# A transformer block on one core: the order of sums at a unit's end, the place of the first weight loads of an item, and the shape of the last part

## The chip, the cores and the metric

The kernel runs on one core of one Trainium2 chip. Its time is the device time of one execution in microseconds (us). The core has five engines that work side by side, each through its own instructions in order: TensorE (PE in the profile; its weight loads are PEld), VectorE (DVE), ScalarE (ACT), GpSimd (POOL) and SyncE (SP). POOL, SP and ACT also issue DMA transfers, each on its own queue. Engines wait for each other by semaphores; an instruction that waits holds up all that stand behind it on its engine.

## The reference

One transformer block with conditioning, for 2 batch items of 2048 tokens with C = 576 channels, 16 heads of 36 channels, all in float32:

```python
ada = silu(c) @ W_ada + b_ada
shift_msa, scale_msa, gate_msa, shift_mlp, scale_mlp, gate_mlp = split(ada, 6)
h = layernorm(x) * (1 + scale_msa) + shift_msa
q, k, v = split(h @ W_qkv + b_qkv, 3)               # 16 heads of 36
x = x + gate_msa * (softmax(q @ k.T / 6) @ v @ W_proj + b_proj)
h = layernorm(x) * (1 + scale_mlp) + shift_mlp
x = x + gate_mlp * (gelu(h @ W_fc1 + b_fc1) @ W_fc2 + b_fc2)   # 2304 hidden columns
```

## The kernel before

**Front.** The modulation, and the queries, keys and values of batch item 0, are computed first and stored to scratch tensors in device memory (`qk_d`, `v_d`). Gates are multiplied into W_proj and W_fc2, which also go to scratch. This takes some 330 us and the change doesn't touch it.

**Attention units.** The main part is a loop over 128 units: 8 blocks of 512 query tokens (4 for each batch item) times 16 heads. A unit has four groups g = 0 to 3 of 512 keys. One step G of the loop does, for groups of different units that overlap: `scores` (16 matmul instructions into two PSUM tiles `s`, L496) and their copy into `e` by ScalarE (`keep`, L509); `exps` (L555, ScalarE); the subtraction of the row maximum `m` (`less`, L551, VectorE); the running maxima `acc` (L514, VectorE); and `weigh`, the values (L567), which sums into the one PSUM tile `av`. Scores are eight groups ahead of values. At g = 0 TensorE turns the finished maxima of a later unit (`turn`, `mt`, L532), VectorE reduces them (`mx`, L542), and SP stores and loads them as `m`. At g = 3 `take` moves `av` out of PSUM: ScalarE copies one half into `up` (L579) and VectorE adds the other (L580). Only then can the next unit's first `weigh` write `av`. A step later `store` writes `up` to `o_d`, half by SP and half as an accumulating DMA by POOL (L588, L589), which waits for SP's to land.

**Other work.** Between scores and values a step may take one piece of other work from a list (`fill`), written as generators. A counter of matmul time (`credit`) decides whether a step takes one: at even g always, at odd g when the credit is over 2.55. The list holds first the projections of batch item 1 (`projections`, four items, `pq` L770 and `pv` L732), then for each of the 8 blocks, once its 16 heads are done, `block(k)`: the output projection into `po` (`begin(k)`, L887) with the residual sum into `x_b` (L899) and layer norm statistics (L102, L103), the first MLP matmuls `pf` (`up_to`, L970 and L956), gelu in three parts (`gT` L981, then L990 and L992, then the later half L998 and L1000, deferred by a list `later` that `flush` works off), and the second MLP matmuls in three parts `down(0)` to `down(2)` of four row tiles each (`py`, L1020), summed into `x_b` (L1032) and at the end stored (L1035). `begin(k + 1)` runs inside `block(k)`, between the last `pf` and `down(2)`, if its heads are done. A piece's PSUM result is moved out by a closure that `fill` returns in `dones`. At the end of a step the order is: `take` if g = 3, then `flush`, then `dones`.

**PSUM and buffers.** While attention runs, other work uses two PSUM banks (`ps_f`); a po, py or pv row tile takes both, one for each half of its 576 columns, and the next such tile waits until the sums have freed them. After attention, `room` gives the two tiles of the scores out as well. `up` and `av` have one buffer each. The weights of `pq` and of `pf` share two buffers (tag `w1`); one set of 256 columns is three DMAs on POOL's queue (`load_cols` with L613, L614, L616; `load_w1` with L867 and twice L870). `x_b` tiles are loaded by POOL (`load_x`, L636), four DMAs for a block.

**The lines around the change.** `projections` loads its first two weight sets when its item begins; `block` loads its first two when the block begins, behind `begin`. The last unit ends near 3592 us; what follows is other work alone, the remainder of block 6 and block 7.

Of the kernel before, what the change touches and what calls it, by code (L numbers as in the profile page):

```python
# [22 lines left out]
def dit_block_kernel(  # L23
# [408 lines left out]
    with ExitStack() as main_part:  # L432
# [175 lines left out]
        def load_cols(key, w, bias, lo, n):  # L608

            t = mp.tile([P, KC, 2 * P], F32, tag="w1", name=f"w1_{key}_{lo}")  # L610
            main, last = pieces(w)
            cols = ds(lo, n)
            seq(nc.gpsimd.dma_start(out=t[:, 0 : KC - 1, :n], in_=main[:, :, cols]))  # L613
            seq(nc.gpsimd.dma_start(out=t[0:KL, KC - 1, :n], in_=last[:, cols]))  # L614
            seq(
                nc.gpsimd.dma_start(out=t[KL : KL + 1, KC - 1, :n], in_=bias[cols].unsqueeze(0))  # L616
            )
            return t
# [71 lines left out]
                yield cost if lights else 1.0, take  # L690

        made = {}

        def tokens(b, tb):

# [14 lines left out]
        def projections(b, tb):  # L710

            key = f"q{b}_{tb}"
            wv = load_square("v", (w_qkv[:, 2 * C :], b_qkv[2 * C :].unsqueeze(0)))
            pairs = [(m, min(2, 2 * C // P - m)) for m in range(0, 2 * C // P, 2)]
            ws = {m: load_cols(key, w_qkv, b_qkv, m * P, n * P) for m, n in pairs[:2]}
            if key not in ready:
                ready[key] = turned(key, made.pop(key), 0, b)
                lights.extend(ready[key][1])
            last = tb == NQB - 1
            yield from lit()  # L720
            hT = ready.pop(key)[0]

            def next_ready():

                return len(work) > 1 and work[1][0] is None

            def values(i):
                pv = room(f"pv_{key}_{i}")
                for n in range(2):
                    for kc in range(KC):  # L730
                        seq(
                            nc.tensor.matmul(  # L732
                                pv[n][:, :C2],
                                lhsT=hT[: rows(kc), kc, ts(i, P)],
                                rhs=wv[: rows(kc), kc, ts(n, C2)],
                                start=(kc == 0),
                                stop=(kc == KC - 1),
                            )
                        )

                def take():
                    t = mp.tile([P, 2 * QB], F32, tag="gT", name=f"vt_{key}_{i}", bufs=5)
                    vt = t[:, : H * HA].rearrange("p (n h e) -> p n h e", n=2, h=H // 2)
                    seq(nc.vector.memset(vt[:, :, :, 0:1], 1.0))
                    for n in range(2):
                        src = pv[n][:, :C2].rearrange("p (h d) -> p h d", d=D)
                        seq(nc.scalar.copy(vt[:, n, :, 1:HA], src))
                    seq(
                        nc.gpsimd.dma_start(
                            out=v_d[b][ts(tb * TB + i, P), :], in_=t[:, : H * HA]  # L750
                        )
                    )

                return 4.95, take

            if last:
                for i in range(TB):
                    step = values(i)
                    if i == TB - 1:
                        squares(0)  # L760
                    yield step
            steps = []
            for at, (m, n) in enumerate(pairs):
                w = ws.pop(m)
                ev = mp.tile([P, 2, QB], F32, tag="gT", name=f"ev_{key}_{m}", bufs=5)
                for j in range(n):
                    pq = room(f"pq_{key}_{m}_{j}", 1)[0]
                    for kc in range(KC):
                        seq(
                            nc.tensor.matmul(  # L770
                                pq,
                                lhsT=w[: rows(kc), kc, ts(j, P)],
                                rhs=hT[: rows(kc), kc, :],
                                start=(kc == 0),
                                stop=(kc == KC - 1),
                            )
                        )

                    def take(m=m, n=n, j=j, src=pq, ev=ev, f=steps.pop(0) if steps else None):
                        by = SCALE if m + j < C // P else qscale if m + j == C // P else 1.0  # L780
                        seq(nc.scalar.activation(ev[:, j, :], src, AF.Copy, scale=by))
                        if j == n - 1:
                            to = qk_d[b][ds(m * P, n * P), ts(tb, QB)]
                            seq(
                                nc.gpsimd.dma_start(
                                    out=to.rearrange("(j p) q -> p j q", p=P), in_=ev[:, :n, :]
                                )
                            )
                        if f is not None:
                            f()  # L790

                    if j == n - 1 and at + 2 < len(pairs):
                        m2, n2 = pairs[at + 2]
                        ws[m2] = load_cols(key, w_qkv, b_qkv, m2 * P, n2 * P)
                    yield 4.27, take
                if last and at + 3 == len(pairs) and next_ready():
                    yield from begin(0)
                    steps = list(begun[0][1])
            if last:
                return  # L800
            for i in range(TB):
                yield values(i)
                if i == 0 and next_ready():
                    to = f"q{b}_{tb + 1}"
                    ready[to] = turned(to, made.pop(to), 0, b)
                    lights.extend(ready[to][1])

# [100 lines left out]
        def block(k):  # L908


            b, qb = divmod(k, NQB)
            if k not in begun:
                yield from begin(k)
                flush()
                for f in begun[k][1]:
                    f()
            x2s, _, xns = begun.pop(k)
            w1s = {f: load_w1(k, f) for f in (0, 2)}
            w2m = w2_d[b].rearrange("(f p) n -> p f n", p=P)
            w2s = {}  # L920

# [89 lines left out]
            def down(part):  # L1011

                f0 = part * per
                for i in range(TB):
                    py = room(f"py_{k}_{part}_{i}")
                    for n in range(2):
                        for j in range(per):
                            f = f0 + j
                            seq(
                                nc.tensor.matmul(  # L1020
                                    py[n][:, :C2],
                                    lhsT=gTs[f - f % 2][:, f % 2, ts(i, P)],
                                    rhs=w2s[f - f % 2][:, f % 2, ts(n, C2)],
                                    start=(j == 0),
                                    stop=(j == per - 1),
                                )
                            )

                    def add(i=i, py=py):
                        for n in range(2):  # L1030
                            to = x2s[i][:, ts(n, C2)]
                            seq(nc.vector.tensor_add(to, py[n][:, :C2], to))  # L1032
                        if part == NT3 - 1:
                            seq(
                                nc.gpsimd.dma_start(  # L1035
                                    out=out[b, ts(qb * TB + i, P), :], in_=x2s[i]
                                )
                            )

                    if i == TB - 1:  # L1040
                        for f in range(f0 + per, min(NF, f0 + 2 * per), 2):
                            load_w2(f)
                    yield 5.94, add

            for f in range(0, NF, 2):
                yield from up_to(f)
# [1 line left out]
                    yield from down(f // per - 1)  # L1048
            steps = []
            if len(work) > 1 and work[1][2] == k + 1 and work[1][0] is None:  # L1050
                yield from begin(k + 1)
                steps = list(begun[k + 1][1])
            else:
                flush()
# [57 lines left out]
        for G in range(-AHEAD, NU * NG + 1):  # L1112
# [39 lines left out]
            else:  # L1152
                subtract(G + 2)
                if tiles:
                    units[su].maxima(sg)
            if 0 <= G < NU * NG and g == NG - 1:
                units[u].take()
            flush()
            for done in dones:
                done()  # L1160
            advance()
            if 0 <= G < NU * NG and g == NG - 1:

# [67 lines left out]
```

## Time and profile before

| | |
|---|---|
| median of 3 runs | 3847.03 us (3845.86 to 3847.26) |
| the profiled execution, its own time | 3850.33 us |
| its span in the profile | 3848.6 us |
| TensorE busy | 3791.6 us, 99% |
| VectorE, ScalarE, POOL busy | 2936.6, 2340.9, 568.5 us |
| `av` and `s` matmuls, busy | 981.8 and 979.0 us |
| `py`, `pf` (L970), `po`, busy | 585.1, 532.1, 167.9 us |
| bytes moved | 362.6 MB, 94 GB/s in the mean |

All times are us from the start of the span, unless a row says otherwise. In a row of waits, the engine and tile that waited come first, then what it waited for, the sum, the number of times and the longest. In the chain of waits a row is a start, a length and what ran. In a timeline row the start and length come first, then engine, line, operation, what it writes and reads, and a count; idle time before it stands in brackets. The granted clock (PEclk) is 1.00 at full speed.

### The profile page before, as it was taken

Reading aid. Unit: us, or ns where it says so; the run is one execution under the profiler, and the core shown is the slowest. Engines: PE = TensorE matmul, PEld = TensorE weight load, DVE = VectorE, ACT = ScalarE, POOL = GpSimd, SP = SyncE. Lnnn points to the kernel's source line nnn. Section 1 sums busy time; section 2 is a strip of 40 time slices with the busy share of each in tenths; the row PEclk is TensorE's granted clock in tenths of the full one; section 3 lists DMA queues with packets and bytes.
Section 4 is the critical chain, followed back from the end, with each engine's and each line's share of the span. In section 5 each row is a group of like instructions: output and inputs, shape, how many; then the busy total and the mean of one; then the engine's idle time right before and its main releaser. Section 6 shows DMA issues by size and latency. Waiting matters only on the chain.

```text
span 3848.6 us, 58305 instructions
## 1 busy us (share of the span) xinstructions
PE 3791.6 (99%) x23533; PEld 1806.7 (47%) x23533; DVE 2936.6 (76%) x2983; ACT 2340.9 (61%) x2203; POOL 568.5 (15%) x821
## 2 busy tenths in 40 slices
PE   8999999999999999999999999999999999999998
PEld 5554434444344444444444534454444444444555
DVE  2514787878888988898888898888888888888421
ACT  0003776766766776676776676667666767677321
POOL 0210111111111011111111021112110111011211
PEclk9998999999999999999999999999999999999999
DMA  5732443344444343343343343434342434243321
GB/s 167 255 136 69 87 99 94 87 116 88 104 86 93 69 95 85 85 88 88 69 102 90 70 112 69 99 71 105 74 102 63 105 80 93 68 102 63 104 82 57
DMA packets 415473, 362.60 MB, mean 94 GB/s; under 512 B 312762, under 2 KB 312762, under 8 KB 415204
## 3 DMA queue, kind: packets, MB, share of 16 engines
q1 hardware_dynamic: 350900, 173.37, 22.8%
q0 software_dynamic: 62000, 180.78, 15.6%
q10 hardware_dynamic: 2304, 4.72, 0.4%
q8 instruction: 186, 3.05, 0.4%
q14 instruction: 83, 0.68, 0.1%
HBM read 287.52 MB, written 71.21 MB: 93 GB/s over the span
## 4 chain that ended last, share of the span: by engine, by line
PE 93%; issue 4%; DMA 1%; DVE 1%; POOL 1%; ACT 0%; SPq 0%; POOLq 0%; ACTq 0%
PE av L567 23%; PE s L496 23%; PE py L1020 13%; PE pf L970 12%; PE pq_q L770 4%; PE pq L208 4%; PE po L887 4%; PE pv_q L732 2%; PE pv L231 2%; PE pf L956 2%; PE mt L532 2%; PE pa L288 1%; PE pg L318 1%; PE pt_b L677 0%; PE pt_q L677 0%
## 5 line engine op out<-in xcount | busy, mean ns | idle before, releaser
L509 ACT COPY e<-s 128x1024 f32<-128x1024 f32 x1024 | 989.7, 1024 | 690.4 <-PE s L496 688.7
L551 DVE TENSOR_TENSOR e<-e,m 128x2048 f32<-128x2048 f32 x512 | 1162.2, 2274 | 7.4 <-DMA m<-m_d 7.4
L514 DVE TENSOR_TENSOR acc<-acc,e 128x1024 f32<-128x1024 f32 x768 | 939.0, 1223 | 213.1 <-ACT e L509 169.0
L555 ACT ACTIVATE e<-e 128x2048 f32<-128x2048 f32 x512 | 992.0, 1938 | 9.4 <-DVE e L551 9.4
L567 PE MATMUL av<-e,v 64*64 64x512 f32 x8192 | 981.8, 594 | 0.6 <-DVE up L580 0.6
L496 PE MATMUL s<-qT,kT 36*64 36x512 f32 x8192 | 979.0, 592 | 0.8 <-ACT vt L245 0.8
L1020 PE MATMUL py<-w,gT 128*128 128x288 f32 x2304 | 585.1, 412 | 6.7 <-DVE gT L1000 3.5
L496 PEld LDWEIGHTS s<-qT,kT 36*64 36x64 f32 x8192 | 311.0, 133 | 561.7 <-issue 519.8
L567 PEld LDWEIGHTS av<-e,v 64*64 64x64 f32 x8192 | 291.5, 132 | 525.5 <-issue 475.5
L970 PE MATMUL pf<-h_b,w_b 128*128 128x512 f32 x1152 | 532.1, 606 | 4.4 <-DMA w_b<-in_L_cond_W_fc_dram 4.4
L1020 PEld LDWEIGHTS py<-w,gT 128*128 128x128 f32 x2304 | 434.4, 191 | 184.9 <-issue 36.8
L588 POOL DMA_DIRECT2D o_d<-up x128 | 110.0, 859 | 2239.2 <-DMA o_d<-up 1286.1
L970 PEld LDWEIGHTS pf<-h_b,w_b 128*128 128x128 f32 x1152 | 208.5, 190 | 323.6 <-issue 308.1
L542 DVE TENSOR_REDUCE mx<-mt 128x4 f32<-128x512 f32 x128 | 88.2, 689 | 200.5 <-PE mt L532 199.8
L981 ACT ACTIVATE gT<-pf,b 128x512 f32<-128x512 f32 x144 | 99.0, 687 | 189.7 <-PE pf L956 131.5
L887 PE MATMUL po<-wpr_p,oT 128*128 128x288 f32 (+1 forms) x640 | 167.9, 419 | 6.3 <-DVE x_b L899 6.3
L770 PE MATMUL pq_q<-h_q,w_q 128*128 128x512 f32 (+1 forms) x360 | 167.0, 611 | 6.5 <-DMA w_q<-in_L_cond_W_qkv_dram 6.5
L208 PE MATMUL pq<-hT,w_in 128*128 128x512 f32 (+1 forms) x360 | 161.8, 607 | 0.3 <-ACT hT L136 0.2
L514 DVE TENSOR_TENSOR acc<-e 128x1024 f32<-128x1024 f32 x128 | 155.4, 1214 | 4.7 <-ACT e L509 4.7
L992 DVE SCALAR_TENSOR_TENSOR th<-th,gT 128x1024 f32<-128x1024 f32 x72 | 88.1, 1223 | 90.9 <-ACT th L990 90.7
L887 PEld LDWEIGHTS po<-wpr_p,oT 128*128 128x128 f32 (+1 forms) x640 | 122.3, 195 | 62.4 <-issue 11.0
L1032 DVE TENSOR_TENSOR x_b<-py,x_b 128x288 f32<-128x288 f32 x192 | 81.5, 451 | 85.9 <-PE py L1020 85.8
(136 smaller groups left out, 2336.0 us busy)
## 6 DMA issues: line engine op xcount, KB each, us to landing
w<-w_d POOLq DMA_DIRECT2D x72, 576.0 KB, 6.2
v<-v_d SPq DMA_DIRECT2D x128, 296.0 KB
kT<-qk_d SPq DMA_DIRECT2D x256, 144.0 KB
w_b<-in_L_cond_W_fc_dram POOLq DMA_DIRECT2D x72, 512.0 KB, 4.5
m<-m_d SPq DMA_DIRECT2D x128, 256.0 KB
qT<-qk_d SPq DMA_DIRECT2D x256, 72.0 KB
w_d<-wg POOLq DMA_DIRECT2D x12, 864.0 KB, 6.3
qk_d<-ev SPq DMA_DIRECT2D x36, 256.0 KB
```

Of the source, the lines that this page charges most:

```text
L208: nc.tensor.matmul(pq, lhsT=w_in[: rows(kc), kc, ts(m, P)], rhs=hT[: rows(kc), kc, :], start=(kc == 0), stop=(kc == KC - 1),)
L496: nc.tensor.matmul(s[ts(c, 64), i, :], lhsT=self.kT[at, ds((2 * g + j) * P + 64 * c, 64)], rhs=self.qT[at, :], start=True, stop=True,)
L509: seq(nc.scalar.copy(self.es[g][:, j], s))
L514: top = lambda out, x, y: seq(nc.vector.tensor_max(out, x, y))
L551: seq(nc.vector.tensor_sub(e, e, m))
L555: seq(nc.scalar.activation(e, e, AF.Exp))
L567: nc.tensor.matmul(self.av[ts(i, 64), r, :], lhsT=self.v[ts(r, 64), ds((c + i * (HALF // P)) * HA, 64)], rhs=e[ts(r, 64), j, i, :], start= ...
L588: seq(nc.gpsimd.dma_start(out=o, in_=hi[1:HA, :], accum_op=ALU.add))
L770: nc.tensor.matmul(pq, lhsT=w[: rows(kc), kc, ts(j, P)], rhs=hT[: rows(kc), kc, :], start=(kc == 0), stop=(kc == KC - 1),)
L887: nc.tensor.matmul(po[n][:, :C2], lhsT=oT[: rows(kc), kc, ts(i, P)], rhs=wpr[: rows(kc), kc, ts(n, C2)], start=(kc == 0), stop=(kc == KC - 1),
L970: nc.tensor.matmul(pfs[j], lhsT=w1[:, kc, ts(j, P)], rhs=h2[:, kc, :], start=(kc == 0 and j == 0), stop=(kc == KC - 2 and j == 1),)
L1020: nc.tensor.matmul(py[n][:, :C2], lhsT=gTs[f - f % 2][:, f % 2, ts(i, P)], rhs=w2s[f - f % 2][:, f % 2, ts(n, C2)], start=(j == 0), stop=( ...
```

## The change

At a unit's end `take` now comes after `flush` and `dones`, so on ScalarE and VectorE the deferred half of gelu and the sums of other work stand ahead of the copy and the addition into `up`.

The first two weight sets of a projection item are loaded while the first values tile of the item in front has just been issued. Those of a block are loaded ahead of `begin` in the block in front (blocks 1 to 7), so on POOL's queue they stand ahead of the `x_b` loads of that block.

In the last block's last part two row tiles begin side by side: both go through the first four of their six weight rows ahead of the last two. That block's output is stored in column halves by SP's queue, each half behind its sum, where before POOL stored whole rows.

```diff
+        early = {}
+        pairs = [(m, min(2, 2 * C // P - m)) for m in range(0, 2 * C // P, 2)]
+
+        def first_cols(key):
+            return {m: load_cols(key, w_qkv, b_qkv, m * P, n * P) for m, n in pairs[:2]}
...
-            ws = {m: load_cols(key, w_qkv, b_qkv, m * P, n * P) for m, n in pairs[:2]}
+            ws = early.pop(key) if key in early else first_cols(key)
...
             for i in range(TB):
                 yield values(i)
+                to = f"q{b}_{tb + 1}"
+                if i == 0:
+                    early[to] = first_cols(to)
...
             if k not in begun:
+                early[k] = {f: load_w1(k, f) for f in (0, 2)}
                 yield from begin(k)
...
-            w1s = {f: load_w1(k, f) for f in (0, 2)}
+            w1s = early.pop(k) if k in early else {f: load_w1(k, f) for f in (0, 2)}
...
             def down(part):
 
                 f0 = part * per
-                for i in range(TB):
-                    py = room(f"py_{k}_{part}_{i}")
+
+                def weigh(i, py, lo, hi):
                     for n in range(2):
-                        for j in range(per):
+                        for j in range(lo, hi):
                             f = f0 + j
...
-                    def add(i=i, py=py):
-                        for n in range(2):
-                            to = x2s[i][:, ts(n, C2)]
-                            seq(nc.vector.tensor_add(to, py[n][:, :C2], to))
-                        if part == NT3 - 1:
+                def add(i, py):
+                    for n in range(2):
+                        to = x2s[i][:, ts(n, C2)]
+                        seq(nc.vector.tensor_add(to, py[n][:, :C2], to))
+                        if part == NT3 - 1 and k == NB - 1:
+                            seq(
+                                nc.sync.dma_start(
+                                    out=out[b, ts(qb * TB + i, P), ts(n, C2)], in_=to
+                                )
+                            )
+                        elif part == NT3 - 1 and n == 1:
                             seq(
                                 nc.gpsimd.dma_start(
                                     out=out[b, ts(qb * TB + i, P), :], in_=x2s[i]
                                 )
                             )
 
+                at = 0
+                if part == NT3 - 1 and k == NB - 1:
+
+                    at = 2
+                    pys = [room(f"py_{k}_{part}_{i}") for i in range(at)]
+                    for lo, hi in ((0, per - 2), (per - 2, per)):
+                        for i in range(at):
+                            weigh(i, pys[i], lo, hi)
+                    yield 11.88, lambda: [add(i, pys[i]) for i in range(at)]
+                for i in range(at, TB):
+                    py = room(f"py_{k}_{part}_{i}")
+                    weigh(i, py, 0, per)
                     if i == TB - 1:
                         for f in range(f0 + per, min(NF, f0 + 2 * per), 2):
                             load_w2(f)
-                    yield 5.94, add
+                    yield 5.94, lambda i=i, py=py: add(i, py)
...
             if len(work) > 1 and work[1][2] == k + 1 and work[1][0] is None:
+                early[k + 1] = {f: load_w1(k + 1, f) for f in (0, 2)}
                 yield from begin(k + 1)
...
-            if 0 <= G < NU * NG and g == NG - 1:
-                units[u].take()
             flush()
             for done in dones:
                 done()
+            if 0 <= G < NU * NG and g == NG - 1:
+                units[u].take()
             advance()
```

## The prediction

> **What bounds the kernel now.** I read the page's busy times first, then TensorE's waits, then the chain of waits around the longest of them, the granted clock in those stretches, and last the timeline where the change puts transfers ahead of others.
>
> ```profile
> PE 3791.6 (99%) x23533; PEld 1806.7 (47%) x23533; DVE 2936.6 (76%) x2983; ACT 2340.9 (61%) x2203; POOL 568.5 (15%) x821
> ```
>
> TensorE is busy 99% of the span, and the change leaves out no matmul. Only its idle time can be won, and its matmuls' speed where that is below the usual. Its waits:
>
> ```profile
> PE pq_q L770 <- DMA w_q<-in_L_cond_W_qkv_dram: 6.5, 1, 6.5
> PE po L887 <- DVE x_b L899: 6.3, 4, 1.6
> PE pf L970 <- DMA w_b<-in_L_cond_W_fc_dram: 4.4, 1, 4.4
> PE py L1020 <- DVE gT L1000: 3.5, 1, 3.5
> PE py L1020 <- DVE x_b L1032: 3.1, 2, 1.6
> ```
>
> Five rows, 23.8 us, 0.6% of the time. How one of the 1.6 us waits comes about, in the chain of waits:
>
> ```profile
> 2108.22 5.05 PE po L887 x20
> ...
> 2115.22 0.58 ACT up L579
> 2115.81 0.97 ACT th L998
> 2116.80 1.22 DVE gT L1000
> 2118.02 0.38 DVE x_b L899
> 2118.45 6.65 PE po L887 x20
> ```
>
> The first row tile of po is done at 2113.3, and its sum into x_b frees the two banks that the second needs. But it stands behind the copy of `up`, and that waits until TensorE ends the unit's values at 2115.2. Also, the second po takes 6.65 us, the same 20 matmuls as 5.05 before. The clock tells why (columns: stretch, its length, PE busy, PEclk, DMA):
>
> ```profile
> 2117.00:2121.70 4.70, 3.25 (x7) 0.64 0.00 0
> 2927.20:2932.00 4.80, 3.23 (x17) 1.00 0.00 0
> ```
>
> After the wait at 2117 the granted clock fell to a half for one stretch; after the equal wait at 2927 it didn't. The half clock shows behind five of the six 1.57 us waits, and behind the three longer ones.
>
> **The change part by part.**
>
> **Sums ahead of a unit's values.** In the changed program's order of instructions something goes ahead of `up` at 38 of 128 unit ends. At six it is the sum of a py or po tile, the six waits above. There tanh L998 no longer stands behind `up`, ScalarE is free by 2111.2, so gT L1000 follows the last maximum (ends 2113.1) until 2114.3, and the first half of the sum ends at 2114.7. The matmuls want the bank at 2118.45 - 1.57 = 2116.9: the wait goes, with 2 us to spare. Idle won: 6.3 + 3.1 = 9.4. The clock: 6.65, 6.81, 5.12 and 6.80 for po, which else takes 5.05, and 7.68 and 7.77 for py, which else takes 6.02: 1.60 + 1.76 + 0.07 + 1.75 + 1.66 + 1.75 = 8.6. Sum 18.0.
>
> A rule speaks against the second half. The Trainium skill (TensorE: Matmul & The Clock Gate, "Why this matters for your kernels") says to avoid TensorE gaps over about 3 us, and under "What's actually happening" it ties the half clock to an idle window of about 3.4 us. By it 1.57 us costs itself alone, and this part wins 9.4. The rows show the half clock behind waits of 1.57, so I take 18.0.
>
> What it costs: `up` is summed later, and the next unit's first values (av) wait for it. Ahead of it go, at most unit ends, L998 (1.06) on ScalarE and L1000 (1.22) on VectorE; at five also a bank add (0.75). From the end of `up` to the next av the timeline leaves 2.9 us at most of these ends, 4.4 at the five, 7 to 10 at the six, and 1.30 at the tightest (2018.2 to 2019.5). 1.22 fits everywhere, at the tightest with 0.1. Cost nothing; if that cover is gone, what exceeds it per unit end.
>
> **w_q loads an item earlier.** Six DMAs on POOL's queue move ahead of three stores of values; their buffers are free, since the item's last pq is through. The wait of 6.54 goes, and 6.06 - 4.49 = 1.57 of half clock. h_q, the other operand, is ready at 632.9, and the matmuls can start at 637.4. Won 8.1.
>
> **w_b loads ahead of begin.** For the last item the wait of 4.37 goes, and 5.40 - 3.70 = 1.70 of half clock; the h_b pieces then arrive ahead of the matmuls that use them. Won 6.1. Items 1 to 6 had no wait here, so nothing to win. But in all seven the six DMAs now stand ahead of the four x_b loads on POOL's queue, and the first sum of po needs x_b:
>
> ```profile
> 1299.69 2.82 POOL L636 DMA_DIRECT2D x_b<-in_x_dram  x4
> ...
> 1303.79 0.82 DVE L899 TENSOR_TENSOR x_b<-po,x_b 128x288 f32<-128x288 f32 x2
> ...
> 1310.24 0.69 DVE L514 TENSOR_TENSOR acc<-acc 128x512 f32<-128x512 f32 x1
> ...
> 1314.42 0.63 PE L532 MATMUL mt<-ident,acc 128*128 128x128 f32 x4
> ```
>
> In items 1 and 2 the x_b loads start late, behind a store that waits; the first lands 3.8 us after its issue, at 1303.45, and is used at once. What two sets of such weights in front cost, the trace shows at the w_q place: w_q is issued from 638.40 on, and then
>
> ```profile
> L636 POOL DMA_DIRECT2D x_q<-in_x_dram x1: 1185/1185/1185, 642.0 to 642.0; - x1
> ...
> DMA to landing us min/median/max: 6.1/6.1/6.1
> ```
>
> so x lands at 648.2, 9.8 after the first weights were issued; a store of 0.7 stood in that queue, so 9.1 to 9.8. Hence x_b lands near 1309.2, and the sum starts 5.4 later than 1303.79. Behind it on VectorE stand its statistics, a subtraction, the maxima and `up`. The last maximum ends at 1310.93 + 5.4 = 1316.3; the transposes mt need it. The second po waits 0.35 for its bank, mt would then start at 1314.8, and waits 1.6. With the half clock in five of six (1.7 x 5/6 = 1.4) that is 3.4, twice: 6.8 lost. Bounds: x_b landing by 1307.6 costs nothing; each us later than 1309.2 costs one more.
>
> In items 3 to 6 the loads start earlier. The first x_b landed at 2106.8; with some 7 us of weights ahead it is 2113.8. The sum could start at 2114.3, and TensorE wants the bank at 2116.9: some 2.5 us to spare. Item 7: w_b waits for the last pf at 3641.9, x_b lands near 3648, its sum was at 3647.3; the fourth po wants that space only at 3656. Nothing.
>
> **The last part.** Before, eight matmuls (3812.58 on) precede the first use of the last gT, which is ready at 3818.16. With two row tiles it is 2 x 2 x 4 x 2 = 32 matmuls at 0.2425 us, 7.8 us, until 3820.3. The wait of 3.53 goes, and the slow start with it: the 88 matmuls took 23.17, as against 21.35 for the 88 at 3773.3, so 1.82. Won 5.35. Behind the last matmul (3841.4) come 0.82 of sums, POOL's DMA 0.29 later, its landing 2.37 later, and the end of the span 3.65 after that, of which POOL's drain (5.25, begun with its last DMA) holds up the others. With SP's queue: 0.82 + 0.05 + a landing between 1.42 (the small m_d store) and 2.37, I take 2.0, + 0.69 of SP's waits + 0.79 of the closing barrier = 4.35 in place of 7.17. Won 2.8; 0.5 if POOL's drain stays as long, 3.4 at best.
>
> **Sum.** 18.0 + 8.1 + 6.1 + 5.35 + 2.8 = 40.4 won, 6.8 lost, net 33.6. The profiled execution's own time, 3850.33 (span 3848.6 and 1.7 around it), becomes 3816.7. The median of the runs is 3.3 below that execution, so 3847.03 becomes 3813.4, 0.87% less.
>
> **The rivals.**
>
> *x_b isn't late enough to matter.* 3847.03 - 40.4 = 3806.6. For it: the queue gave x_b 3.8 us alone, and the maxima leave 3.5 us before mt. Against: 9.1 to 9.8 us behind equal loads. Chance 0.13.
>
> *x_b later than reckoned, in items 3 to 6 too.* If it lands over 2.5 us later than 2113.8, the four po waits return, with 6.3 + 5.2 = 11.5, and items 1 and 2 lose 2.5 more each: 3813.4 + 16.5 = 3830. For it: attention's small transfers share the engines. Chance 0.16.
>
> *Slower: av waits for `up`.* One mechanism, at the some 30 unit ends where tanh and gT now precede `up`. Slower by 0.2% needs 33.6 + 7.7 = 41.3 us, 1.4 at each end, so 2.9 + 1.4 = 4.3 us of moved work; the rows give 1.22. With 1.7 at each: 3813.4 + 51 = 3864. Chance 0.05.
>
> *It doesn't do what it says.* The order of instructions shows that it does; but if the gains come back as other waits, since VectorE has 76% of the span busy and loses its pauses, some 6 us or less remain: within 0.2%, chance 0.03.
>
> **How the numbers follow.** My forecast has 0.63, itself within 3808 to 3820: the clock in items 1 and 2 and the end of the kernel give or take 3 each. With the two rivals near it 0.92 lies under 3839. The range 3804 to 3829 takes in the first rival and most of the second. A difference of 0.2%, 7.7 us, is about what a measurement of this kernel can tell from none. Faster 0.92, same 0.03, slower 0.05.
>
> **What would show it.** The rows po <- x_b and py <- x_b, w_q, w_b and gT gone from TensorE's waits, and every po and py near 5.05 and 6.02; mt waiting for the maxima near 1310 and 1715, after a sum of x_b that waits for its DMA; the end within 5 us of the last matmul. Wrong would be: waits of av for `up` in rows, po still waiting in items 3 to 6, or a half clock where there was none.

## The result, and the profile after

The median of five runs went from 3847.26 us (3845.86 to 3852.21) to 3811.77 us (3809.58 to 3816.51): ratio 0.9907 [0.9892, 0.9921], 35.5 us less. The forecast was 3813.4. The profiled execution of the changed kernel took 3811.77 itself, with a span of 3810.0. In the profile of the kernel before, whose span is 3848.6, the front took 3.1 us longer than here, ahead of any code that the change touches; the remaining 35.5 of the 38.6 between the spans are the change.

The busy times and TensorE's longest waits on the page and in the view of waits of the changed kernel (the tile that waited, what it waited for, sum, number, longest):

```profile
PE 3777.2 (99%) x23533; PEld 1797.4 (47%) x23533; DVE 2935.9 (77%) x2983; ACT 2343.4 (62%) x2203; POOL 567.1 (15%) x817
```
```profile
PE pt_c L268 <- ACT c_in L265: 13.9, 1, 13.9
PE mt L532 <- DVE acc L514: 2.8, 2, 1.6
...
PE av L567 <- DVE up L580: 1.2, 1, 1.2
```

The number of matmuls is the same, and their busy sum is 14.4 lower. Of that, 11.7 lies behind the front: it is the half clock that no longer follows the waits. The other 2.8 lies in the front, where the half clock differs from profile to profile. The five rows of 23.8 us (w_q, po, w_b, gT, py) are all gone. The row pt_c is the kernel's start and was there before. New are two waits of `mt` for the maxima, and the wait of `av` for `up` has grown to 1.16 from 0.61, in the kernel before:

```profile
PE av L567 <- DVE up L580: 0.6, 1, 0.6
```

The place of block 3's second po tile, in the chain of waits of the changed kernel (start, length, what ran):

```profile
2095.57 5.05 PE po L893 x20
...
2104.22 5.05 PE po L893 x20
2109.27 0.47 PE mt L532 x4
2109.74 1.88 PE av L567 x16
```

Between the two tiles stand only values and scores; no tanh, no `gT`, no copy of `up` is left on the path. The second po takes 5.05, where it took 6.65 before.

What was lost shows at block 1, in the timeline of the changed kernel (start, length, engine, line, operation; the idle time before it in brackets):

```profile
1285.47 1.43 POOL L873 DMA_DIRECT2D w_b<-in_L_cond_W_fc_dram  x1
...
1289.55 1.36 POOL L636 DMA_DIRECT2D x_b<-in_x_dram  x2
...
1294.61 0.82 DVE L905 TENSOR_TENSOR x_b<-po,x_b 128x288 f32<-128x288 f32 x2 [5.02 <-DMA x_b<-in_x_dram]
...
1301.05 0.69 DVE L514 TENSOR_TENSOR acc<-acc 128x512 f32<-128x512 f32 x1
...
1301.89 0.72 PE L532 MATMUL mt<-ident,acc 128*128 128x128 f32 x4 [1.60 <-DVE acc L514]
...
1302.53 3.24 PE L567 MATMUL av<-e,v 64*64 64x512 f32 x16
```

The first `x_b` tile landed at 1294.51, 9.04 after the first of the weights was issued. VectorE stood still for 5.02 us, its maxima were late by that, and TensorE's transposes waited 1.60. The 16 values behind them took 3.24; the same row elsewhere shows 1.95. The granted clock of that stretch says why (stretch, length, busy times of PE, PEld, DVE, ACT and POOL with counts, then PEclk, DMA share, GB/s):

```profile
1303.05:1306.46 3.41, 3.41 (x24) 1.05 (x20) 3.41 (x4) 0.00 (x0) 0.00 (x0) 0.50 0.05 5
```

This is the only stretch of half clock that begins between the front and the last matmul. In block 2 the same wait is 1.23 and no half clock follows.

The sum of these entries, in the two first profiles: 23.9 of waits gone, 13.7 of half clock gone behind them (8.6 at the six short waits, 1.57, 1.70 and 1.82 at the three long ones), 3.3 less behind the last matmul (7.17 to 3.87); against that 2.83 of `mt`, 0.55 more of `av`, and 1.7 of half clock. Net 35.8, where the spans give 35.5.

### The profile page after: what moved, and what is told of

It is laid out like the page before. It is cut to its first block, busy times and chain, and to the rows that moved or that the text cites. A ratio compares the mean times of both kernels' runs of the same rounds, so it can differ in the third digit from the quotient of the medians.

```text
span 3810.0 us, 58326 instructions
## 1 busy us (share of the span) xinstructions
PE 3777.2 (99%) x23533; PEld 1797.4 (47%) x23533; DVE 2935.9 (77%) x2983; ACT 2343.4 (62%) x2203; POOL 567.1 (15%) x817
## 4 chain that ended last, share of the span: by engine, by line
PE 96%; DMA 1%; DVE 1%; issue 1%; POOL 0%; ACT 0%; SPq 0%; ACTq 0%; DVEq 0%; POOLq 0%
PE av L567 23%; PE s L496 23%; PE py L1027 15%; PE pf L977 13%; PE pq_q L774 4%; PE pq L208 4%; PE po L893 4%; PE pv_q L736 2%; PE pf L963 2%; PE pv L231 2%; PE mt L532 2%; PE pa L288 1%; PE pt_b L677 1%; PE pg L318 1%; DVE acc L514 0%
## 5 line engine op out<-in xcount | busy, mean ns | idle before, releaser
L589 POOL DMA_DIRECT2D sum_d<-up x128 | 144.3, 1128 | 0.7 <-issue 0.7
```

The costliest lines, as they stand in the source:

```text
L589: seq(nc.gpsimd.dma_start(out=sums, in_=hi[0:1, :], accum_op=ALU.add))
```

## The experiments

The theory was the forecast's: each part takes away one wait and the half clock behind it, and the weights ahead of `x_b` cost something in blocks 1 and 2. The rivals were that the order of sums and `up` doesn't matter, that the loss isn't from the place of the `x_b` loads, and that the gains hang on each other. Of the medians below, those that share a chip are compared where that is said. The kernel before, run beside them, had medians of 3848.76, 3847.69 and 3847.76 on the three chips, so the chips differ by about 1 us. The medians themselves are less certain than that: the changed kernel's own runs spread over 7 us, and each ratio's interval is 11 to 13 us wide. Much of that spread can come from the front, which no edit here touches: in the thirteen profiles it takes 340.9 to 346.7 us, with half clock for 27.5 to 41.7 of them.

So the profiles' time behind the front, from the first of batch item 1's query matmuls (tile `pq_q`) to the end of the span, stands beside the medians in the table behind the experiments. It is 3504.6 in the kernel before and 3505.1 in its second profile, and 3469.1 and 3466.0 in the two of the changed kernel, which is 35.5 and 39.1 less.

**The x_b loads ahead of the weights.** `begin` loads the four `x_b` tiles first and the two weight sets after them, at both places that call it; all else is the changed kernel.

```diff
-        def begin(k):
+        def begin(k, first=False):
...
             x2s = load_x(f"b{k}", b, qb)
+            if first:
+                early[k] = {f: load_w1(k, f) for f in (0, 2)}
...
-                early[k + 1] = {f: load_w1(k + 1, f) for f in (0, 2)}
-                yield from begin(k + 1)
+                yield from begin(k + 1, True)
```

> The changed kernel, but the x_b loads of a block stand ahead of its first two weight sets on POOL's queue. My theory, that x_b behind the weights makes the maxima and so the transposes mt late in items 1 and 2: both mt waits (1.6 and 1.2) go, the half clock behind them goes, VectorE no longer waits 5 us for x_b; some 2.8 to 4.5 us less than the changed kernel's 3811.8, about 3808. Rival, that mt waits because VectorE now has more ahead of `up` at a unit's end: mt still waits 2.8, time as before the edit.

Median 3811.15 (3808.91 to 3812.43), ratio 0.9902 [0.9887, 0.9916]. The row of the sum of po, in the groups of VectorE, of the changed kernel and then of this one (busy, mean ns | idle before, what ended it):

```profile
L905 DVE TENSOR_TENSOR x_b<-po,x_b 128x288 f32<-128x288 f32 x64 | 26.1, 448 | 18.7 <-DMA x_b<-in_x_dram 10.0 <-PE po L893 8.7
```
```profile
L907 DVE TENSOR_TENSOR x_b<-po,x_b 128x288 f32<-128x288 f32 x64 | 26.2, 449 | 8.8 <-PE po L895 8.7
```

The 10.0 us for the DMA are gone, and with them both `mt` waits and the half clock. From the first `pq_q` matmul to the last matmul of the kernel, a stretch called the main part from here on, the profiled execution takes 3460.8, and 3465.2 in the changed kernel: 4.4 less. The waits of `mt` and their half clock come to 1.60 + 1.23 + 1.7 = 4.5, but the last `av` wait is 0.7 longer here:

```profile
PE av L567 <- DVE up L580: 1.9, 1, 1.9
```

The other 0.6 of the 4.4 is matmul time for which no cause was found. The medians differ by only 0.6, where about 3 to 4.5 were expected: in the runs of the changed kernel the loss can be smaller than in its first profile (the last experiment shows one such). So the `mt` waits come from the `x_b` loads' place; that they cost anything in the median is not shown.

**`up` ahead of the other work's sums again.** One move undone:

```diff
+            if 0 <= G < NU * NG and g == NG - 1:
+                units[u].take()
             flush()
             for done in dones:
                 done()
-            if 0 <= G < NU * NG and g == NG - 1:
-                units[u].take()
```

> The changed kernel with `up` ahead of the deferred work and the sums again. My theory: the six waits of 1.57 return (9.4 us idle) and most bring a half clock of 1.7, so 15 to 19 us more than 3811.8, about 3829; the two mt waits stay at 1.2 to 1.6. Rival by the clock rule[...]: 9.4 more, about 3821, and no stretch of half clock behind the waits. Rival that `up` behind the sums makes mt late: the mt waits go.

Median 3822.83 (3820.72 to 3825.54), ratio 0.9933 [0.9918, 0.9948]; 11.1 over the changed kernel, 11.7 over the one above on the same chip. The waits of this kernel, and the chain at the po tile shown above:

```profile
PE po L893 <- DVE x_b L905: 6.3, 4, 1.6
PE py L1027 <- DVE x_b L1039: 3.1, 2, 1.6
```
```profile
2108.68 0.58 ACT up L579
2109.26 0.97 ACT th L1005
2110.23 0.02 issue
2110.25 1.23 DVE gT L1007
2111.48 0.38 DVE x_b L905
2111.86 0.04 issue
2111.90 5.12 PE po L893 x20
```

All six waits are back, to the hundredth, and with the same chain. But this po takes 5.12, not 6.65: five of the six waits are not followed by half clock. So the time is nearer to the rival's 3821 than to 3829, with one such stretch where the rival had none. Two stretches behind waits of the same 1.57 us, in the columns used above:

```profile
2113.40:2119.00 5.60, 5.60 (x35) 3.78 (x38) 3.40 (x3) 0.45 (x1) 0.00 (x0) 1.00 0.01 3
2920.70:2926.00 5.30, 5.30 (x20) 4.01 (x19) 1.82 (x1) 0.33 (x1) 0.00 (x0) 0.78 0.00 0
```

The `mt` waits did not stay at 1.2 to 1.6; they are 0.55 and 0.44, just under what the six other profiles with `x_b` behind the weights and in its order have (0.57 to 1.65). The rival that `up` behind the sums has some part in them is not excluded.

So the move is worth 9.4 of idle time in all three profiles with `up` first and, here, 1.7 of clock; the 8.6 of the forecast belongs to the kernel it was read from.

**`up` between the two.** The sums of po and py stand behind `up`, the deferred half of gelu ahead of it.

```diff
             flush()
-            for done in dones:
-                done()
             if 0 <= G < NU * NG and g == NG - 1:
                 units[u].take()
+            for done in dones:
+                done()
```

> The changed kernel with `up` between the two: the deferred half of gelu ahead of it, the sums of other work behind it. If the sums must stand ahead of `up`, the six waits return with 1 us or more. My reading of the chain, in which `up`, tanh, gT and the sum stood in a row: with tanh and gT taken out of that row, `up` ends at 2116.5 and the first half of the sum at 2116.9, when the matmuls want the bank, so the six waits come to 0 to 0.2, and the time is within 1 us of 3811.8: then the order of `up` and gelu is what won, not that of `up` and the sums.

Median 3812.76 (3809.63 to 3818.82), ratio 0.9913 [0.9898, 0.9928]. No wait of po or py. At the same po tile, in the timeline of this kernel:

```profile
2102.11 1.22 DVE L1007 SCALAR_TENSOR_TENSOR gT<-th,gT 128x1024 f32<-128x1024 f32 x1
...
2104.32 0.59 ACT L579 COPY up<-av 128x512 f32<-128x512 f32 x1 [3.11 <-PE av L567]
2104.94 0.69 DVE L580 TENSOR_TENSOR up<-up,av 128x512 f32<-128x512 f32 x1 [1.61 <-ACT up L579]
...
2105.54 0.81 DVE L905 TENSOR_TENSOR x_b<-po,x_b 128x288 f32<-128x288 f32 x2
...
2106.05 5.12 PE L893 MATMUL po<-wpr_p,oT 128*128 128x288 f32 x20
```

`up` is summed ahead of `x_b`, and po starts without waiting. What had held the sum was not `up` itself (0.58 and 0.69) but tanh and `gT`, 1.0 and 1.2 us, that were released only behind it. Moving gelu is enough for the gain of this part, within the 1.0 between the medians; the sums ahead of `up` with gelu behind it were not run.

**The first w_q weights late.** The projections load them when the item begins, as before.

```diff
                 to = f"q{b}_{tb + 1}"
-                if i == 0:
-                    early[to] = first_cols(to)
```

> The changed kernel with the first weights of a projection item loaded at its own beginning again. My theory: the wait for w_q returns with 6.5 us and its slow matmuls with 1.6, about 3820. Rival, that the early loads only moved the wait: within 2 us of 3811.8.

Median 3819.09 (3817.42 to 3822.52), ratio 0.9925 [0.9909, 0.9942], 7.3 over the changed kernel. Waits of this kernel:

```profile
PE pq_q L774 <- DMA w_q<-in_L_cond_W_qkv_dram: 6.5, 1, 6.5
```

The wait is back with 6.46, and half clock from 638.0 on.

**The block's weights late.** Both places that load them ahead of `begin` are taken out, so `x_b` is first in all blocks and block 7 waits for its weights.

```diff
-                early[k] = {f: load_w1(k, f) for f in (0, 2)}
                 yield from begin(k)
...
-                early[k + 1] = {f: load_w1(k + 1, f) for f in (0, 2)}
                 yield from begin(k + 1)
```

> The changed kernel with a block's first weights loaded behind begin again. My theory: the last item's wait for w_b returns (4.4, and 1.7 of slow matmuls), both mt waits go (1 to 2.8, and their half clock): 1 to 5 more than 3811.8, about 3815. If the early loads cost nothing: 6 more, about 3818.

Median 3818.31 (3816.80 to 3820.00), ratio 0.9924 [0.9907, 0.9941]; 6.5 over the changed kernel. That is the number of the rival, that the early loads cost nothing, and not the theory's 3815; the waits of this kernel tell the two apart:

```profile
PE pf L976 <- DMA w_b<-in_L_cond_W_fc_dram: 4.3, 1, 4.3
...
PE av L567 <- DVE up L580: 2.0, 1, 2.0
```

The 4.32 of block 7 and its half clock are back, and the `mt` waits are gone, as in the theory. Of the surplus over the expectation, 1.7 is a half clock behind the `av` wait of 2.02, which the changed kernel doesn't have.

**The x_b tiles loaded in reverse.** The tile that is needed first is the last of the four in the queue.

```diff
-        def load_x(key, b, qb):
+        def load_x(key, b, qb, back=False):
...
-            for i in range(TB):
+            for i in range(TB)[:: -1 if back else 1]:
...
-            return xs
+            return xs[:: -1 if back else 1]
...
-            x2s = load_x(f"b{k}", b, qb)
+            x2s = load_x(f"b{k}", b, qb, True)
```

> The changed kernel with the four x_b loads of a block issued last tile first, so that the tile that the first sum of po needs is the fourth behind the weights instead of the first and lands some 2.2 later (1296.68 in place of 1294.51 in the changed kernel's trace). My theory, one us later is one us of wait once the maxima's slack is used: the two mt waits, 0.4 to 1.6 so far, grow to 2.6 to 3.8, half clock behind most; in items 3 to 6 the sum is just reached (2.5 to spare by the prediction), so po waits there 0 to 0.3. In all 5 to 8 more than 3811.8, about 3818. Rival, no margin in items 3 to 6: four po waits of over 1 return, about 3825.

Median 3817.94 (3815.79 to 3820.55), ratio 0.9925 [0.9910, 0.9939]; 6.2 more than the changed kernel. Waits of this kernel:

```profile
PE po L893 <- DVE x_b L905: 3.9, 2, 2.2
...
PE mt L532 <- DVE acc L514: 1.6, 1, 1.6
```

The time came as expected, its place only in part: in blocks 1 and 2 the second po now waits for its bank, 1.71 and 2.19, ahead of `mt`, which waits 1.65 in block 1 and not at all in block 2. Behind the 2.19 the clock is half for 6.83, two stretches. A later `x_b` costs, then, and first at whichever consumer comes first. In blocks 3 to 6 there is still no wait of po, with the tile later than in the changed kernel.

**One row tile after the other in the last part.** The stores by SP stay.

```diff
                 at = 0
-                if part == NT3 - 1 and k == NB - 1:
...
-                    yield 11.88, lambda: [add(i, pys[i]) for i in range(at)]
                 for i in range(at, TB):
```

> The changed kernel, but the last part goes row tile by row tile again; its output still leaves by SP in halves. My theory: the wait for the last gT returns with 3.5 us and the slow matmuls behind it with 1.7, so 5.3 more, about 3817; the end of the span stays within 4 us of the last matmul. Rival by the idle time alone: 3.5 more.

Median 3816.83 (3815.59 to 3818.23), ratio 0.9917 [0.9902, 0.9932]; 5.1 over the changed kernel. The wait of this kernel, 3.53 until 3786.8, with half clock from 3786.1 on:

```profile
PE py L1027 <- DVE gT L1007: 3.5, 1, 3.5
```

The half clock lasts 6.83 here, and 3.41 behind the same wait in the kernel before, while the `mt` waits come to 1.3 without half clock, in place of 2.8 with it. So that 5.1 is near the forecast's 5.35 is in part chance.

**The last block stored by POOL.** Whole rows, behind the second half's sum, as before; two row tiles still go side by side.

```diff
-                        if part == NT3 - 1 and k == NB - 1:
...
-                        elif part == NT3 - 1 and n == 1:
+                        if part == NT3 - 1 and n == 1:
```

> The changed kernel, but the last block's output leaves by POOL's queue in whole rows again; the two row tiles still begin side by side. My theory, that POOL's drain behind its last DMA holds up the end: from the last matmul to the end of the span 7.2 instead of 3.9, so 3.3 more, about 3815 and hard to tell in the times; TensorE's waits as in the changed kernel. Rival, that only the landing counts: 0.7 more.

Median 3817.61 (3816.32 to 3821.13), ratio 0.9922 [0.9907, 0.9937]. From the last matmul to the end of the span 7.20 us, with SP's queue 3.87. The ends of the two chains, of this kernel and then of the changed one:

```profile
3802.68 0.54 POOL out_dram L1042
3803.22 5.26 issue
3808.47 0.56 POOLq L1246
```
```profile
3799.80 6.32 PE py L1027 x26
3806.12 0.02 issue
3806.14 0.46 DVE x_b L1039
3806.60 0.36 DVEq L1252
```

The chain no longer ends on POOL: from its last DMA to its last step there it has 5.26 us between, in this run as in the kernel before. The profiled executions differ by 3.3 at the end; the medians on one chip by 5.5 (to the last experiment), of which one `mt` wait of 1.65 with half clock and a 2.02 wait of `av` are in the profile.

**A buffer of its own for one `up`.** In the changed kernel's chain the `av` wait of 1.16 hangs on the copy of `up`, which waits for the accumulating store of the previous one, since `up` has one buffer. To the kernel with `x_b` loaded first, this adds a free buffer for the `up` of the unit next to the last.

```diff
-                self.up = np_.tile([P, QB], F32, tag="up", name=f"up_{self.u}", bufs=1)
+                if self.u == NU - 2:
+                    t = kp.tile([P, HALF], F32, tag="kT", name=f"up_{self.u}")
+                    self.up = t[:, :QB]
+                else:
+                    self.up = np_.tile([P, QB], F32, tag="up", name=f"up_{self.u}", bufs=1)
```

> x_b ahead of the weights as in the first experiment, and unit 126's `up` in a buffer of its own (one of the keys, which are used up by then), so that it needn't wait until the unit in front is stored. If that store is what made the last wait of av for `up` grow from 0.6 to between 1.2 and 2.0: it falls to 0.7 or less, and no mt wait is left; 3 to 5 less than the changed kernel on the same chip, about 3808. If `up` waits for VectorE's subtractions instead: the wait stays over 1.

Median 3808.02 (3806.68 to 3808.50), ratio 0.9895 [0.9880, 0.9910]. The wait didn't fall as expected; it is 1.39. The chain of waits of this kernel there:

```profile
3541.48 4.47 DMA m<-m_d
3545.95 0.02 issue
3545.97 0.04 DVE e L551
3546.01 2.17 issue
3548.18 0.75 DVE x_b L949
3548.94 2.20 DVE e L551
3551.14 0.61 DVE up L584
3551.75 0.04 issue
3551.79 3.66 PE av L567 x32
```

The store is out of the chain. What remains is VectorE's order: the sum of `up` stands behind a subtraction that began late because the maximum `m` came late from memory. The buffer was one of two causes that end close together, and taking one away left the other. With the `x_b` loads it is nevertheless the best version seen: 4.05 under the changed kernel's median on the same chip, and its slowest run lies under that one's fastest. How much of that is the buffer isn't told apart by the times; in the profiles the main part is 3460.7, as good as the 3460.8 with `x_b` first alone, so nothing of the buffer shows in the whole.

**The kernel before and the changed kernel again.** Both without an edit, for a second profile.

> The kernel before, once more, for its clock. If a wait of 1.57 us brings the half clock by itself: behind five or six of the six waits again, and behind w_q, w_b and gT. If it depends on when the wait falls: another number of the six, while the three waits over 3.4 us always bring it.

The kernel before: 3848.63, 3497.9 from the first `pq_q` matmul to the last (3497.4 in the first profile). Again five of the six waits of 1.57 are followed by half clock, and again the one near 2927 isn't.

> The changed kernel once more, beside the one above: mt waits of 0.4 to 1.6 in items 1 and 2, some with the half clock, av's last wait 1.2 to 2.0, six waits gone; 3809 to 3817.

The changed kernel: median 3812.07 (3811.69 to 3818.22), ratio 0.9911 [0.9895, 0.9928]. Its `mt` waits are 0.68 and 0.83, without half clock, and its main part 3462.1, 3.1 less than in its first profile. So the price of the late `x_b` differs from execution to execution, here by 0.9 and 0.4 in the waits and by whether 1.7 of half clock follows.

## Why the prediction was right, step by step

The time came out 1.6 under the forecast. Not each term did. The last column has the change's worth by time behind the front, from the two profiles of the changed kernel:

| step | forecast, us | shown by | measured, us | behind the front, us |
|---|---|---|---|---|
| sums ahead of a unit's values | -18.0 | `up` first again | -11.1 by medians; -18.0 in the first trace | -7.9, -11.1 |
| w_q an item earlier | -8.1 | w_q late | -7.3 by medians | -5.7, -8.8 |
| w_b ahead of `begin`, block 7 | -6.1 | w_b late | -6.0 by the trace (4.32 + 1.7) | -3.6, -6.7, net of the next row |
| x_b behind the weights, blocks 1 and 2 | +6.8 | x_b first | +4.5 in the first trace, 1.5 in the second; +0.6 by medians | +4.4, +1.2 |
| two row tiles side by side | -5.35 | one by one | -5.1 by medians | -3.9, -7.0 |
| the end | -2.8 | POOL's store | -3.3 by the trace | -3.3 of -4.2, -7.4 |

**Sums ahead of a unit's values.** Idle 9.4 was right, with its chain. For the clock, the term "1.60 + 1.76 + 0.07 + 1.75 + 1.66 + 1.75 = 8.6" was read off correctly and repeats in the second profile of the kernel before, but it isn't a property of a 1.57 us wait: the same six waits in a kernel whose other parts were shortened cost 1.7 in all. The forecast had nothing to tell which case its step would meet, so that the term held there is luck. The rule of the Trainium skill that was weighed there (TensorE: Matmul & The Clock Gate, "Why this matters for your kernels": no gaps over about 3 us) would have given 9.4 for this part; with 8.6 less of gain, and 2.8 less of loss behind the `mt` waits, which are as short, that is 3819.2 in all, against 3813.4 forecast and 3811.8 measured. For this part alone, the runs lie between the two readings: a wait well under 3 us may halve the clock, and need not. And the step described what moves as the sums; the experiment with `up` between shows that moving gelu alone is enough.

**Weights earlier.** Both long waits went as worked out. In block 1 `x_b` landed 9.04 after the first weights' issue, in block 2 9.3, at the low end of the 9.1 to 9.8 forecast or just under it; `mt` waited 1.60 and 1.23, forecast 1.6. Too large were the half clock (1.4 each; one of two) and the 0.35 of the second po, which didn't wait. In blocks 3 to 6 `x_b` landed 1.55 to 2.4 before its use, so the rival with a wait there had no place.

**The last part and the end.** 5.35 and 5.1 agree, by the trace in part by chance. The end took 3.87, the forecast said 4.35 between bounds.

**`av` waits.** "Cost nothing" held at 127 of 128 unit ends. At the last but one the wait grew from 0.61 to between 1.16 and 2.02 in the versions with `up` late, and is 0.54 with `up` first. The forecast took 1.30 as the tightest cover and didn't look at this end, where TensorE already waited in the kernel before, and where nothing stands ahead of `up` that didn't before. In the changed kernel's trace the copy of `up` waits for the store of the previous `up`, here in this kernel's chain and in that of the kernel before:

```profile
3550.24 3.71 DMA sum_d<-up
```
```profile
3574.42 1.76 DMA sum_d<-up
```

Without that, the late `m` holds it. That `up`'s place brings this about is shown, how it does so is not.

So the sum stands for the step from the kernel before to this one: 33.6 forecast, 35.5 measured. The loss was 2.3 too large in the first trace (6.8 to 4.5), the end 0.5 too small, and `av` cost 0.55 that wasn't entered, together 2.2. The second profiles differ by 39.1, mostly because the `mt` waits are shorter there and bring no half clock; so a total within 1.6 us of the forecast is in part luck. The single undoings give 11.1 + 7.3 + 6.5 + 5.1 + 3.3 = 33.3 (w_b net of its loss), which the medians can't tell from 35.5. What the first part would bring to the kernel before by itself was not run.

## What to carry to other kernels

Where a deferred step is released by an engine's wait, move the deferred step ahead of the waiting instruction: the six waits were paid for gelu behind `up`, not for `up`. When a load is moved earlier, look at what stands behind it in the same queue and put the smaller, sooner needed one first. And a clock loss behind a short wait is to be entered as a range from nothing to what the trace shows, since another edit may remove it for free.

## What was not expected of the hardware

Behind the front, half clock came in stretches of 3.41 us, or of twice that, and their starts lie on a grid of 3.413 us through an execution: in the kernel before at 640.20, 1210.22, 1616.41 and 2118.17, which is 167, 119 and 147 steps from one to the next. Whether an idle time of TensorE brought one depended on its place in that grid. Of the eighteen waits of 1.57 in the two profiles of the kernel before and the one with `up` first, those that began 0.87 to 2.11 us after a grid point (eleven) were all followed by half clock, and those that began 0.05 to 0.69 or 2.39 to 3.04 after one (seven) were not. The two profiles of the kernel before have nearly the same places, so these are not eighteen independent cases; but it fits that the same wait costs 1.6 more at one place and nothing at another, and that edits elsewhere change it. Waits up to 1.39 were never followed by half clock, and those over 3.4 always. It is no full rule: of ten other waits, of 1.60 to 2.19, five agree with it and two began outside the three ranges. Three do not agree: the changed kernel's 1.60 began at 0.65 and was followed by half clock, and waits of 2.02 went both ways, with half clock from 0.22 and without from 1.67.
